# Two graph layers on one core: which pairs' later layers run beside the last sort, and how far ahead their gathered rows are asked for

## The chip, the cores and the metric

One core of a Trainium2 chip runs the whole program. The number that counts is the device time of one execution in microseconds. The engines are named as in the profile: PE is TensorE (matrix products), PEld its weight loads, DVE is VectorE, ACT is ScalarE, POOL is GpSimd and SP is SyncE, which here only issues transfers. A name with a q behind it (SPq, POOLq) is the sequencer of that engine, where DMAs are issued.

## What is computed

Sixteen graphs of 1024 nodes with 64 channels go through two layers. Layer 0 takes the ReLU of a layer norm, drops some edges by a rule on the degree, and takes for every node and channel a weighted sum of three quantiles over the values of its neighbours; a small network with 128 hidden units follows. Layer 1 is three graph convolutions, whose outputs are joined and multiplied once more. Both layers add their result to their input.

```python
def reference(x, adj, nodemask, ...):
    # layer 0
    h = max(layernorm(x), 0)
    nd   = edges of adj left after dropping, with the node itself
    s    = sort(where(nd, h[neighbours], inf))            # per node and channel
    agg  = sum over (tau, w) of w * quantile(s, tau)      # 0.25, 0.5, 0.75
    y    = relu((h + agg) @ W1 + b1) @ W2 + b2
    x    = x + y * mask
    # layer 1
    h  = max(layernorm(x), 0)
    x1 = bn(relu(adj @ (h  @ W1) + b1))
    x2 = bn(relu(adj @ (x1 @ W2) + b2))
    x3 = bn(relu(adj @ (x2 @ W3) + b3))
    x  = x + relu(concat(x1, x2, x3) @ Wl + bl)
```

## The kernel before, in words

The graphs are handled as eight pairs, 0 to 7, two graphs side by side. Three kinds of work follow each other for a pair.

- Preparation: the adjacency is read, edges are dropped, nodes are put in the order of their degree and the places of the nodes in that order are kept in `place`.
- The sort. Nodes in order of degree fall into seven blocks of columns (`BLOCKS`) and a tail. For each block PE gathers the neighbours' values into `g` (line 1018), and DVE runs a network of minima and maxima on it (line 935) and weighs the rows (941, 950). The aggregates are turned by PE (1043), copied by ACT and written to DRAM (`agg_d`), in degree order.
- The later layers, in `later`. `first(p)` is the rest of layer 0. It loads `xt`, `h` and the mask on SP's queue (lines 1240, 1241 and 1249), and gathers the rows of `agg_d` by the indices of `place` with sixteen indirect DMAs of 128 rows on POOL's queue (line 1243). Then DVE adds `agg` and `h` (1142), PE turns the sum (1131) and ACT copies it (1134), two products with ReLU follow for each graph (1151, 1152, 1155, 1156), the mask and the skip connection (1158, 1159), a layer norm (560 to 568, with ACT at 563 and 566), and again a turn into `chan`. `second(p)` is layer 1: it loads the two adjacencies `adjT` (1259), and for each of three convolutions makes the product with the weights (1184), splits it into three bf16 parts (ACT 1185 and 1189, DVE 1188 and 1190), multiplies by the adjacency in two halves of 48 products (1200), and finishes each half on ACT (1204) and DVE (1205). The last product is line 1216, the end is on DVE (1220, 1223), and SP writes the result (1225).

Generators weave these kinds together: `Steps` wraps a generator whose `yield`s are its steps, and `weave(sort, (steps, count, ...))` takes `count` steps spread over the sorting of one block. While the last pair is sorted, `later` is the work that is woven in, with `STEPS` steps for each of the blocks 0 to 7 (the tail is 7; in block 0 the sort of the tails of pairs 4 to 6 comes after). Inside `later`, `second(p)` and `first(p + 1)` take steps in turn, so that the first layer of the next pair lies beside the convolutions of this one. `first` has one step for its loads and four behind them; `second` has eleven. What is left of the eight pairs when the sorting ends is run by `ahead.rest()`, in the same order.

Buffers come from pools. `late` holds one buffer of each tile of the later layers, two of `xt`; `ps_late` holds two of each kind in PSUM. With one `agg`, the gathers of pair p + 1 wait until PE has turned the `agg` of pair p for the second time (1131). A pool that opens over the space of others waits for those that used it.

The build does not keep the order of the source strictly: it lays the instructions of each engine out in a list of its own, moving some ahead of others by its estimate of when they can run. In the trace each engine works through its list from front to back.

Of the kernel before, what the change touches and what calls it, by code (L numbers as in the profile page):

```python
# [10 lines left out]
F32 = mybir.dt.float32  # L11
# [4 lines left out]
U8 = mybir.dt.uint8  # L16
# [3 lines left out]
PSUM = bass.MemoryType.PSUM  # L20
DRAM = bass.MemoryType.DRAM

P = 128
C = 64
# [4 lines left out]
TAUS = ((0.25, 0.25), (0.5, 0.5), (0.75, 0.25))  # L29

SHARES = (10, 9, 17, 24, 20, 13, 0)
STEPS = 7

MAGIC = 8388608.0

# [366 lines left out]
def graph_layers_kernel(ctx: ExitStack, tc: tile.TileContext, ins, out: bass.AP):  # L402
    nc = tc.nc
    x_d, adj_d, mask_d = ins["x"], ins["adj"], ins["nodemask"]
    NB, N, _ = x_d.shape
    NT = N // P
    HALF = 512
    NH = N // HALF
    NP = NB // 2
# [144 lines left out]
    def rows_of(ap):  # L554
        return ap.rearrange("(t p) c -> p t c", p=P)
# [476 lines left out]
    def send(pools, after=None):  # L1032

        for one in waiting:
            store(*one, pools, after)
        waiting.clear()
# [100 lines left out]
    def first_layer(pools, xt, h, agg, mask):  # L1137


        one, ps = pools  # L1140
        X = xt.shape[2]
        nc.vector.tensor_tensor(agg, agg, h, ALU.add)
        oT = channels_first(pools, agg, "chan")
        yield
        for x in range(X):
            rows = slice(x * C, (x + 1) * C)
            hT = one.tile([HID, N], F32, tag="hT", name="hT")
            for hf in range(NH):
                sl = slice(hf * HALF, (hf + 1) * HALF)
                pm = ps.tile([HID, HALF], F32, tag="mm", name="pm1")  # L1150
                nc.tensor.matmul(out=pm, lhsT=w1[rows, :], rhs=oT[rows, sl], start=True, stop=True)
                nc.scalar.activation(hT[:, sl], pm, AF.Relu, bias=b1)
            py = ps.tile([P, NT, C], F32, tag="mm", name="py")
            for t in range(NT):
                nc.tensor.matmul(out=py[:, t, :], lhsT=hT[:, t * P : (t + 1) * P], rhs=w2, start=True, stop=True)
            nc.vector.tensor_tensor(h[:, :, x, :], py, b2[:, None, :].to_broadcast([P, NT, C]), ALU.add)
            yield
        nc.vector.tensor_tensor(h, h, mask[:, :, :, None].to_broadcast([P, NT, X, C]), ALU.mult)
        nc.vector.tensor_tensor(xt, xt, h, ALU.add)
        flat = "p t x c -> p (t x) c"  # L1160
        layernorm_relu(one, agg.rearrange(flat), xt.rearrange(flat), h.rearrange(flat), NT * X)
        yield
        return channels_first(pools, agg, "chan")
# [61 lines left out]
            nc.sync.dma_start(out=rows_of(graphs[x]), in_=res[:, :, x, :])  # L1225
        yield

    def later(pools, done):

        one, ps = pools  # L1230

        def first(p):
            assert p < done.sent
            xt = one.tile([P, NT, 2, C], F32, tag="xt", bufs=2, name="xt")
            h, agg = (one.tile([P, NT, 2, C], F32, tag=k, name=k) for k in ("h", "agg"))
            mk = one.tile([P, NT, 2], U8, tag="mk", name="mk")
            mask = one.tile([P, NT, 2], F32, tag="mask", name="mask")
            for x in range(2):
                b = 2 * p + x
                nc.sync.dma_start(out=xt[:, :, x, :], in_=rows_of(x_d[b]))  # L1240
                nc.sync.dma_start(out=h[:, :, x, :], in_=rows_of(h_d[b][:, :]))
                for t in range(NT):
                    nc.gpsimd.indirect_dma_start(  # L1243
                        out=agg[:, t, x, :],
                        out_offset=None,
                        in_=agg_d[b][:, :],
                        in_offset=bass.IndirectOffsetOnAxis(ap=place[:, b, t : t + 1], axis=0),
                    )
                nc.sync.dma_start(out=mk[:, :, x], in_=mask_d[b])
            yield  # L1250
            nc.vector.tensor_copy(mask, mk)
            cur = yield from first_layer(pools, xt, h, agg, mask)
            return xt, cur

        def second(p, x2, cur):
            adjT = []
            for x in range(2):
                adjT.append(one.tile([P, NT, N], F8, tag=f"adjT{x}", name=f"adjT{x}"))
                nc.sync.dma_start(out=adjT[x], in_=adjT_d[2 * p + x][:, :, :])
            yield  # L1260
            yield from next_layer(pools, [out[2 * p], out[2 * p + 1]], adjT, x2, cur)

        given = yield from first(0)
        for p in range(NP):
            now = Steps(second(p, *given))
            ahead = Steps(first(p + 1)) if p + 1 < NP else None
            while now.step():
                yield
                if ahead is not None and ahead.step():
                    yield  # L1270
            if ahead is not None:
                ahead.rest()
                given = ahead.result
# [146 lines left out]
    with ExitStack() as stack:  # L1420
        keep = stack.enter_context(tc.tile_pool(name="keep", bufs=1))
        pools = (
            stack.enter_context(tc.tile_pool(name="work", bufs=1)),
            stack.enter_context(tc.tile_pool(name="ps", bufs=1, space=PSUM)),
            stack.enter_context(tc.tile_pool(name="rows", bufs=1)),
        )
        last = len(BLOCKS)
        with ExitStack() as inner:
            early = (
                inner.enter_context(tc.tile_pool(name="early", bufs=1)), keep,  # L1430
                inner.enter_context(tc.tile_pool(name="ps_early", bufs=1, space=PSUM)),
            )
            ahead = Steps(prepare(0, early))
            ahead.rest()
            st = ahead.result
            first, *_ = gather_block(st, 0, pools)
            first.rest()
            for p in range(NP - 1):


                def coming(st, p):
                    yield from st.number
                    return (yield from prepare(p + 1, early))

                ahead = Steps(coming(st, p))
                for n in range(last):
                    steps = (ahead, SHARES[n], 0.0, 1.0)
                    if n == 0 and p in TAILS:

                        tails = sort_tails(*TAILS[p], pools)  # L1450
                        next(tails)
                        weave(sort_block(st, n, pools), steps)
                        weave(tails, gather_block(st, n + 1, pools))
                    elif n == last - 1:
                        ahead.rest()
                        to_come = ahead.result
                        weave(sort_block(st, n, pools), gather_block(to_come, 0, pools))
                    elif n == last - 2:
                        weave(
                            sort_block(st, n, pools), gather_block(st, n + 1, pools),  # L1460
                            gather_block(st, last, pools, (early[0], "a", 2)), steps,
                        )
                    else:
                        weave(sort_block(st, n, pools), gather_block(st, n + 1, pools), steps)
                st = to_come
            for _ in st.number:
                pass


        with ExitStack() as inner:  # L1470
            one = inner.enter_context(tc.tile_pool(name="late", bufs=1))
            late = (one, inner.enter_context(tc.tile_pool(name="ps_late", bufs=2, space=PSUM)))
            done = Pair()
            done.sent = TAILS[NP - 1][0]
            ahead = Steps(later(late, done))
            for n in range(last + 1):
                steps = (ahead, STEPS, 0.0, 1.0)
                if n == 0:
                    tails = sort_tails(*TAILS[NP - 1], pools)
                    next(tails)  # L1480
                    weave(sort_block(st, n, pools), steps)
                    weave(tails, gather_block(st, n + 1, pools))
                    continue
                if n < last:
                    weave(sort_block(st, n, pools), gather_block(st, n + 1, pools), steps)
                else:
                    weave(sort_block(st, n, pools), steps)
                done.sent = NP - 1
            send(pools)
            done.sent = NP  # L1490
            ahead.rest()


    with ExitStack() as stack:
# [43 lines left out]
```

## Time and profile before

| what | us |
|---|---|
| three runs: median (lowest, highest) | 3160.63 (3157.54, 3173.24) |
| the profiled execution: its own time | 3163.56 |
| its span | 3161.8 |
| preparation and sorts of pairs 0 to 6, up to the sort of the last pair | 0 to about 2340 |
| last sort, with the later layers beside it | about 2340 to 2832.2 |
| later layers alone | 2832.2 to 3161.8 |

Results of pairs 0 to 7 are issued to DRAM at 2623.7, 2736.2, 2823.0, 2900.0, 2972.7, 3048.1, 3108.8 and 3155.0 us. So three pairs are finished beside the sort; the fourth is in its first convolution when the sort ends and the fifth in its first layer.

The times of the trace are microseconds from the start of the span; a line of the timeline gives start, duration, engine, line of the code, operation, names, how many, and in brackets the idle time of the engine ahead of it with the work that ended it. A line of the waits says which engine at which line waited for which, the total, how often, and the longest.

### The profile page before, as it was taken

The page shows a single profiled execution, that of the slowest core. Times are in us where ns is not written, and L with a number is a line of the kernel's source. Part 1 is how long each engine was busy: PE and PEld are TensorE (multiplying, and loading weights), DVE is VectorE, ACT ScalarE, POOL GpSimd, SP SyncE. Part 2 cuts the span into 40 slices and gives each one's busy share as a digit, 9 for nine tenths or more (in the row PEclk, how much of TensorE's full clock was granted, in tenths as well). Part 3 has the DMA queues.
Part 4 walks back from the last instruction along what each step waited for, and adds up shares of the span by engine and source line. Part 5 has one row for each costly group of instructions (what it writes and reads, how often), then busy time and mean ns, then how long its engine had stood idle before and what let it go on. Part 6 is the DMA issues. An engine that isn't in the chain of part 4 may idle for free.

```text
span 3161.8 us, 67201 instructions
## 1 busy us (share of the span) xinstructions
PE 2599.2 (82%) x27849; PEld 1697.4 (54%) x27849; DVE 2559.8 (81%) x5895; ACT 1696.2 (54%) x3292; POOL 619.5 (20%) x545
## 2 busy tenths in 40 slices
PE   2678978898888889885798889888986688977778
PEld 1445655565556556653565566456643456644445
DVE  4149889998999799989998999899976979963332
ACT  4764666567557755774367557745853223332221
POOL 5110161022102200330022103300422530311110
PEclk9779999999899999997899999999987799988989
DMA  4131022111211212122111211211113011122211
GB/s 138 46 104 60 3 67 70 56 55 52 66 57 54 64 56 68 46 72 47 42 64 51 66 56 57 67 56 63 48 36 75 9 41 26 49 55 54 54 54 42
DMA packets 221082, 177.45 MB, mean 56 GB/s; under 512 B 189024, under 2 KB 189152, under 8 KB 216672
## 3 DMA queue, kind: packets, MB, share of 16 engines
q1 hardware_dynamic: 141824, 125.88, 13.1%
q0 software_dynamic: 17408, 37.81, 3.9%
q10 hardware_dynamic: 61536, 9.39, 1.7%
q8 instruction: 219, 3.59, 0.5%
q14 instruction: 95, 0.78, 0.1%
HBM read 124.44 MB, written 48.55 MB: 55 GB/s over the span
## 4 chain that ended last, share of the span: by engine, by line
DVE 40%; PE 29%; ACT 12%; DMA 8%; issue 6%; another core or an unknown queue 2%; POOL 2%; ACTq 1%; DVEq 0%; POOLq 0%; SPq 0%
PE pg L1018 11%; DVE t L935 10%; DVE s L987 9%; DVE g L935 8%; PE pg L1200 5%; ACT junk L770 3%; DMA a<-in_adj 3%; DMA lp<-live_d 3%; DVE junk_v L673 2%; PE pr L845 2%; DVE g_tails L935 1%; DVE t_tails L935 1%; PE keys L763 1%; PE pf L1216 1%
## 5 line engine op out<-in xcount | busy, mean ns | idle before, releaser
L1018 PE MATMUL pg<-s,hp 128*64 128x400 bf16 (+11 forms) x16848 | 1366.5, 313 | 172.3 <-DVE s L987 138.1
L1018 PEld LDWEIGHTS <-hp 128*64 128x64 bf16 x16848 | 894.5, 112 | 553.9 <-issue 109.6
L987 DVE TENSOR_SCALAR s<-r 128x3200 bf16<-128x3200 bf16 (+25 forms) x1312 | 623.6, 521 | 103.6 <-PE pg L1018 74.9
L778 POOL DMA_INDIRECT live_d<-edge,place x128 | 261.1, 2040 | 1354.3 <-DVE place L773 1149.9
L1023 ACT COPY g<-pg 128x400 f32<-128x400 f32 (+10 forms) x384 | 169.0, 443 | 399.4 <-PE pg L1018 363.1
L935 DVE TENSOR_TENSOR t<-g 128x600 f32<-128x600 f32 (+9 forms) x524 | 315.5, 626 | 34.0 <-ACT g L1023 33.2
L1200 PE MATMUL pg<-adjT,xw 128*64 128x512 fp8e4 x2304 | 284.5, 398 | 52.8 <-ACT xw L1185 25.7
L935 DVE TENSOR_TENSOR g<-t 128x96 f32<-128x96 f32 (+16 forms) x555 | 283.2, 537 | 1.2
L1243 POOL DMA_INDIRECT agg<-agg_d,place x128 | 171.2, 1338 | 495.2 <-PE pt L1131 258.2
L671 ACT ACTIVATE edge<-a 128x1024 fp8e4<-128x1024 f32 x128 | 135.1, 1058 | 214.4 <-DMA a<-in_adj 213.9
L1200 PEld LDWEIGHTS <-xw 128*64 128x64 bf16 x2304 | 140.1, 114 | 182.4 <-issue 42.0
L868 ACT ACTIVATE coef<-z,bias 128x200 f32<-128x200 bf16 (+6 forms) x480 | 173.9, 405 | 102.3 <-DVE agg L950 66.0
L935 DVE TENSOR_TENSOR t<-t 128x192 f32<-128x192 f32 (+20 forms) x447 | 207.8, 475 | 0.2
L871 ACT ACTIVATE coef<-coef,wcol 128x200 f32<-128x200 f32 (+7 forms) x512 | 189.6, 403 | 9.3 <-issue 7.1
L673 DVE SCALAR_TENSOR_TENSOR junk_v<-a 128x1024 fp8e4<-128x1024 f32 x128 | 155.4, 1214 | 24.4 <-DMA a<-in_adj 24.4
L845 PE MATMUL pr<-liveT,upto 128*128 128x512 fp8e4 (+2 forms) x384 | 127.4, 350 | 53.1 <-ACT r L851 46.9
L770 ACT ACTIVATE junk<-keys,minus 128x1024 fp8e4<-128x1024 f32 x128 | 144.3, 1128 | 38.1 <-PE keys L763 34.3
L851 ACT CAST r<-pr 128x592 bf16<-128x592 f32 (+1 forms) x256 | 142.5, 585 | 41.1 <-PE pr L847 32.1
L794 POOL DMA_DIRECT2D lp<-live_d x128 | 89.4, 699 | 376.9 <-PE pt L809 319.3
L812 ACT ACTIVATE liveT<-pt 128x1024 fp8e4<-128x1024 f32 x128 | 130.3, 1034 | 50.5 <-PE pt L809 47.1
L752 ACT ACTIVATE edge<-q,bias 128x1024 fp8e4<-128x1024 f32 x128 | 141.8, 1108 | 22.6 <-PE q L747 22.6
L725 ACT ACTIVATE stays<-cs,back 128x1024 f16<-128x1024 f32 x128 | 136.7, 1111 | 31.1 <-PE cs L721 15.9
(182 smaller groups left out, 3879.4 us busy)
## 6 DMA issues: line engine op xcount, KB each, us to landing
a<-in_adj SPq DMA_DIRECT2D x128, 512.0 KB
adjT_d<-edgeT SPq DMA_DIRECT2D x16, 1024.0 KB
lp<-live_d POOLq DMA_DIRECT2D x128, 128.0 KB
adjT<-adjT_d SPq DMA_DIRECT2D x16, 1024.0 KB
room<-in_x SPq DMA_DIRECT2D x16, 256.0 KB
h_d<-room SPq DMA_DIRECT2D x16, 256.0 KB
h_again<-h_d SPq DMA_DIRECT2D x16, 256.0 KB
xt<-in_x SPq DMA_DIRECT2D x16, 256.0 KB
```

The costliest lines, as they stand in the source:

```text
L673: nc.vector.scalar_tensor_tensor(junk, a, 1.0, a, ALU.is_equal, ALU.not_equal, accum_out=odd[:, b, t : t + 1], saturate=False)
L770: nc.scalar.activation(junk, keys, AF.Sign, bias=minus[:, t : t + 1], accum_out=above[:, t : t + 1], saturate=False)
L778: sent = nc.gpsimd.indirect_dma_start(out=live_d[b][:, :], out_offset=bass.IndirectOffsetOnAxis(ap=place[:, b, t : t + 1], axis=0), in_=ed ...
L845: nc.tensor.matmul(out=pr[:, o], lhsT=upto, rhs=liveT[:, u, sl], start=True, stop=(u == 0))
L868: nc.scalar.activation(coef[:, i, :], z[:, at], AF.Abs, bias=bias(rank - (slots + 1) // 2 + tau), scale=sign)
L871: nc.scalar.activation(coef[:, i, :], coef[:, i, :], AF.Relu, bias=wcol[:, q : q + 1], scale=-w)
L935: nc.vector.tensor_tensor(view(bufs, o, n1, n2), view(bufs, a, n1, n2), view(bufs, b, n1, n2), ALU.max if op else ALU.min)
L987: nc.vector.tensor_scalar(s[:, k, :, us, w0:], r[:, :, us, at + w0 : at + W], float(LIVE + 1 + k0 + k), None, ALU.is_equal)
L1018: summed = nc.tensor.matmul(out=pg[x * C : (x + 1) * C, ks, w0:], lhsT=st.hp[:, part, x, u, :], rhs=s[:, ks, x, u, w0:], start=(whole and ...
L1023: nc.scalar.copy(g[:, k0 : k0 + n, :], pg)
L1200: nc.tensor.matmul(out=pg[cs, :], lhsT=part[:, u, cs], rhs=adjT[x][:, u, sl], start=(u == 0 and k == 0), stop=(u == NT - 1 and k == len(xw ...
L1243: nc.gpsimd.indirect_dma_start(out=agg[:, t, x, :], out_offset=None, in_=agg_d[b][:, :], in_offset=bass.IndirectOffsetOnAxis(ap=place[:, b ...
```

## The change

Four things change. `STEPS` goes from 7 to 11, but in block 0 of the last sort only one step is taken. `first` puts `LEAD` = 4 empty steps between its loads with the gathers and the first use of them. Only pairs 0 to 3 (`BESIDE`) are given to the `later` beside the sort, and `ahead.rest()` ends them there. Pairs 4 to 7 get a `later` of their own, after the pools of the sort are closed: new pools (`last` with two buffers of each tile and four of `xt`, `h`, `agg` and the mask's bytes, `ps_last` with four PSUM buffers of each kind), in which two series, pairs 4 and 6 and pairs 5 and 7, take steps in turn. In a series (`in_turn`) the loads of the next pair are issued before the layers of this one, and `first` and `second` of one pair follow each other.

```diff
-STEPS = 7
+STEPS = 11
+BESIDE = 4
+LEAD = 4
@@ later
-    def later(pools, done):
+    def later(pools, done, pairs, apart=False):
         one, ps = pools
-        def first(p):
+        deep = dict(bufs=4) if apart else {}
+        def load(p):
             assert p < done.sent
-            xt = one.tile([P, NT, 2, C], F32, tag="xt", bufs=2, name="xt")
-            h, agg = (one.tile([P, NT, 2, C], F32, tag=k, name=k) for k in ("h", "agg"))
+            xt = one.tile([P, NT, 2, C], F32, tag="xt", bufs=4 if apart else 2, name="xt")
+            h, agg = (one.tile([P, NT, 2, C], F32, tag=k, name=k, **deep) for k in ("h", "agg"))
...
-            yield
+            return xt, h, agg, mk
+
+        def first(p, loaded=None):
+            if loaded is None:
+                loaded = load(p)
+                for _ in range(LEAD):
+                    yield
+            xt, h, agg, mk = loaded
+            mask = one.tile([P, NT, 2], F32, tag="mask", name="mask")
             nc.vector.tensor_copy(mask, mk)
             cur = yield from first_layer(pools, xt, h, agg, mask)
             return xt, cur
...
-        given = yield from first(0)
-        for p in range(NP):
+        def in_turn(pairs):
+            ahead = load(pairs[0])
+            yield
+            for i, p in enumerate(pairs):
+                loaded, ahead = ahead, load(pairs[i + 1]) if i + 1 < len(pairs) else None
+                yield from second(p, *(yield from first(p, loaded)))
+
+        if apart:
+            both = [Steps(in_turn(pairs[k::2])) for k in range(2)]
+            while any([one.step() for one in both]):
+                yield
+            return
+        given = yield from first(pairs[0])
+        for p in pairs:
             now = Steps(second(p, *given))
-            ahead = Steps(first(p + 1)) if p + 1 < NP else None
+            ahead = Steps(first(p + 1)) if p + 1 in pairs else None
@@ the last sort
-            ahead = Steps(later(late, done))
+            ahead = Steps(later(late, done, range(BESIDE)))
             for n in range(last + 1):
-                steps = (ahead, STEPS, 0.0, 1.0)
+                steps = (ahead, STEPS if n else 1, 0.0, 1.0)
...
             send(pools)
-            done.sent = NP
             ahead.rest()
+    with ExitStack() as stack:
+        done.sent = NP
+        late = (
+            stack.enter_context(tc.tile_pool(name="last", bufs=2)),
+            stack.enter_context(tc.tile_pool(name="ps_last", bufs=4, space=PSUM)),
+        )
+        Steps(later(late, done, range(BESIDE, NP), True)).rest()
```

More of the change, by code (lines that the diff above doesn't have):

```diff
@@ L1226, in next_layer @@
         yield
-    def later(pools, done):
+    def later(pools, done, pairs, apart=False):
         one, ps = pools
-        def first(p):
+        deep = dict(bufs=4) if apart else {}
+        def load(p):
             assert p < done.sent
-            xt = one.tile([P, NT, 2, C], F32, tag="xt", bufs=2, name="xt")
-            h, agg = (one.tile([P, NT, 2, C], F32, tag=k, name=k) for k in ("h", "agg"))
-            mk = one.tile([P, NT, 2], U8, tag="mk", name="mk")
-            mask = one.tile([P, NT, 2], F32, tag="mask", name="mask")
+            xt = one.tile([P, NT, 2, C], F32, tag="xt", bufs=4 if apart else 2, name="xt")
+            h, agg = (one.tile([P, NT, 2, C], F32, tag=k, name=k, **deep) for k in ("h", "agg"))
+            mk = one.tile([P, NT, 2], U8, tag="mk", name="mk", **deep)
             for x in range(2):
```

## The prediction

> **What bounds the kernel now.** I read the page's totals first, then the waits in two stretches, then the timelines of PE and POOL. The totals name no single bound, since stages differ:
>
> ```profile
> PE 2599.2 (82%) x27849; PEld 1697.4 (54%) x27849; DVE 2559.8 (81%) x5895; ACT 1696.2 (54%) x3292; POOL 619.5 (20%) x545
> ```
>
> The change touches only what follows 2340 us, so I split there. Beside the last sort (2350 to 2834) DVE's own waits are:
>
> ```profile
> DVE agg L1142 <- DMA agg<-agg_d,place: 22.6, 2, 12.6
> DVE xT L1205 <- ACT xT L1204: 18.1, 5, 6.0
> DVE h L1156 <- PE py L1155: 14.1, 6, 5.7
> ```
>
> DVE is the bound there: from 2340 to 2834 all its waits together are 85 us, and the sort's instructions fill the rest. After the sort (2834 to 3162) PE is the bound, with gaps. The windows (columns: PE, PEld, DVE, ACT, POOL busy, then clock and DMA) show a pair with gathers beside it, and one without:
>
> ```profile
> 3006.00:3029.00 23.00, 11.99 (x72) 6.22 (x71) 1.93 (x3) 2.63 (x5) 15.12 (x16) 0.65 0.10 24
> 3080.00:3103.00 23.00, 22.50 (x184) 16.17 (x184) 4.65 (x8) 5.54 (x9) 0.00 (x0) 0.93 0.04 9
> ```
>
> PE halves its work while POOL gathers. The last product of each pair gives the pace:
>
> ```profile
> 2892.40 5.62 PE L1216 MATMUL pf<-wlast,xT 128*128 128x128 f32 x48
> 2965.09 5.62 PE L1216 MATMUL pf<-wlast,xT 128*128 128x128 f32 x48
> 3040.47 5.62 PE L1216 MATMUL pf<-wlast,xT 128*128 128x128 f32 x48
> 3101.16 5.62 PE L1216 MATMUL pf<-wlast,xT 128*128 128x128 f32 x48
> 3147.31 5.62 PE L1216 MATMUL pf<-wlast,xT 128*128 128x128 f32 x48
> ```
>
> The steps are 72.7, 75.4, 60.7 and 46.2 us: with gathers beside, twice; with a first layer but no gathers; alone. So gathers cost about 13 us a pair here and a hidden first layer 14.5. Last, POOL's gathers: the first one of pair 2, beside the sort, and the ends of a set there and of one after the sort.
>
> ```profile
> 2568.96 8.27 POOL L1243 DMA_INDIRECT agg<-agg_d,place  x1 [74.07 <-DVE s L987]
> 2599.25 0.94 POOL L1243 DMA_INDIRECT agg<-agg_d,place  x1 [0.30 <-DMA agg<-agg_d,place]
> 2856.72 0.94 POOL L1243 DMA_INDIRECT agg<-agg_d,place  x1 [57.91 <-PE pt L1131]
> 2875.44 0.95 POOL L1243 DMA_INDIRECT agg<-agg_d,place  x1 [0.30 <-issue]
> ```
>
> Sixteen take 31 us beside the sort (47 for pair 1, 2449.7 to 2497) and 20 after it, 0.94 with 0.30 between.
>
> [...] 1.57 us a gather beside the sort, 0.94 when DVE idles. [...] Here the last gather of pair 0 starts at 2412.47 and DVE goes on at 2415.12, 2.65 us later. [...] four products take 3.71 us at 2418 after a pause, 1.98 at 2916.
>
> **The change part by part.** For the changed kernel I have the lists in which its instructions stand on each engine, and what each waits for, but no times; lines are those of before. Up to the end of the last sort DVE's list holds the same work in both (117 instructions of the later layers before, 116 now: pairs 0 to 2, pair 3 up to its first convolution).
>
> 1. *End of the sort*, 2832.2 before. (a) Pair 0's first layer moves behind the tails' sort: its two waits at line 1156, 3.61 and 5.74 us, go: -9.4. (b) Pair 4's gathers leave this stretch; in 2778 to 2800 DVE was busy 9.8 of 22 us: -12.2. (c) The gathers' waits. The four empty steps don't lengthen the way from release to use: a pair's 19 steps now fill under two blocks, and the release (line 568, then PE's turn 1131) comes late in the pair. Summing DVE's list between line 568 of one pair and line 1142 of the next, at the trace's durations for each shape (0.25 us at 96 columns, 0.98 at 800, linear between), gives 21.7, 18.1 and 23.3 us for pairs 1, 2 and 3; before it was 50.1, 34.5 and 42.6. Against 30 to 47 us of gathers that leaves 5 to 19 us (PE is loaded there and covers part), 15 and 8; pair 0 keeps about 10, since its sum stands right behind its gathers as before. About 45 in place of 22.6: +22. Net 0, with ±20: -46 if every gather wait goes (a, b and all of 22.6), +20 if none of (b) is found.
>
> 2. *Pair 3 alone.* Before, pair 4's first layer lay beside it. Now nothing does: the first loads of the new pools wait for PE's last product of pair 3 and for the landing of its two result stores. From the second convolution on, pair 7 before took 34 us (3121.45 to 3154.95), and stores land about 4.5 us after issue (DMA engines are busy until some 3159.4). 38.7 in all.
>
> 3. *Gathers of pairs 4 to 7.* All 64 stand back to back on POOL, none issued before step 2 ends. 64 x 1.25 = 80, and 2.4 to land. Beside them SP brings 16 loads of 256 KB and four adjacencies of 1 MB; with such loads pair 0's sixteen took 23 us instead of 20, so up to 10 more. I take 86 (82 to 92). What waits: DVE's list has the sum (line 1142) of pair 6 ahead of the second output half of pair 4's first layer, and the sum of pair 7 ahead of pair 4's and 5's variance (565) and normalising (568). DVE can't pass it, so PE gets no convolution until pair 7's rows have landed, although only pairs 4 and 5 need theirs (at 20 and 40 us). The first layers of 4 and 5, some 20 us of PE, are hidden in these 86.
>
> 4. *Chain behind it*: DVE 1.22 + 1.21 + 1.22 + 0.25 + 1.22, PE's turns 1.0, ACT 0.6 twice, the same for pair 5 interleaved, products 1184 and ACT 1185: 11.
>
> 5. *Convolutions of 4 and 5 together.* Twelve halves at 5.4 (the x48 groups of line 1200 at full clock) are 64.8; two later rounds of line 1184, 4.6 each, 9.2; line 1216 twice, 11.3; 2 for a cold start: 87. Handoffs of one pair lie under the other's products; alone a pair would take 46.2.
>
> 6. *First layers of 6 and 7.* They follow line 1216 in PE's list with nothing beside. PE: turns 2.1, then 8 us a pair, 19 with ACT; then DVE's 0.69, eight of 1.2 and small ones, 13, turn and products 3: 35.
>
> 7. *Convolutions of 6 and 7*: 87. *End*: 9.5 (8.9 from line 1216 before).
>
> Sum behind the sort: 38.7 + 86 + 11 + 87 + 35 + 87 + 9.5 = 354. Before: 3161.8 - 2832.2 = 329.6. With step 1 at 0 that is +24.6 on the span. The profiled execution took 3163.56, of which 1.8 lie outside the span, and the median of the three runs is 2.9 below it; I add the difference to the median: 3160.6 + 24.6, about 3185.
>
> **Rivals.** *R1, the gathers' waits lengthen the sort.* For: the short distances of 1c. Against: PE's load may cover them. +20 more: 3205. *R2, the hold at pair 7's rows costs little.* Pair 5 lands at 42 us, its own chain takes 35, so convolutions could not start before 79 in place of 97: -18, 3167, no difference that can be told. For it: DMA could run quicker than I take; against: the list. *R3, faster: rows asked for ahead leave the last sort.* One mechanism, DVE's idle time from 2390 to 2800: if the waits at 1142 (22.6), 1156 (9.4) and in pair 4's window (12.2) all go, the sort ends 44 us sooner: 3141. It decides once it removes more than 40 us (24.6 + 15.8). For: (a) and (b) are sure to move; against: 1c.
>
> **How the numbers follow.** Under 0.5%, 15.8 us, a change in this kernel can't be told from none. Forecast 0.49 (3172 to 3200), R1 0.25, R2 0.18, R3 0.08. Slower: 0.86 of the forecast (0.42), all of R1, a tenth of R2: 0.69. Same: the rest of the forecast and of R2: 0.07 + 0.16 = 0.23. Faster: 0.08. The range takes in R2, R1 with its waits somewhat longer than 20 us, and part of the way to R3: 3154 to 3216.
>
> **What would show it.** After pair 3's result a stretch of some 85 us with PE mostly idle, POOL issuing 64 gathers in a row, and DVE waiting at line 1142 for `agg_d` rows of pairs 6 and 7; then two dense stretches of PE of about 85 us with 35 between them; gathers' waits on DVE beside the sort above 22.6. I am wrong if PE's convolutions start within 60 us of pair 3's store, if the sort ends before 2800, or if POOL's gathers after it take well off 1.25 us.

## The result, and the profile after

The changed kernel is slower. Its median over four runs is 3211.41 us (3205.90 to 3222.38), against 3161.79 (3157.54 to 3173.24) for the kernel before beside it: a ratio of 1.0146, with a 95% interval of 1.0123 to 1.0168. The forecast of 3185 lay 26 us below, and the range (3154 to 3216) holds the result near its upper end.

In the profiled execution (span 3207.2 us, 45.4 more than before) the last sort ends 7.0 us sooner (2825.9 against 2832.8, by the end of PE's last `pt_agg`), and what follows takes 381.3 us instead of 329.0. In code, lines of the later layers now stand four below the old ones, those of the loads six.

Beside the sort, the view of the waits (2340 to 2826; total, times, longest) shows DVE waiting longer for gathered rows:

```profile
DVE agg L1146 <- DMA agg<-agg_d,place: 37.9, 4, 11.5
DVE h L1160 <- PE py L1159: 16.8, 5, 6.9
```

These are the 22.6 and 14.1 of before. Behind the sort the windows show four stretches of the tail (columns as in the prediction):

```profile
2863.00:2898.90 35.90, 9.53 (x28) 6.29 (x28) 1.63 (x3) 2.54 (x4) 26.95 (x28) 0.50 0.81 141
2898.90:2940.30 41.40, 0.00 (x0) 0.00 (x0) 0.03 (x1) 0.00 (x0) 30.56 (x34) 0.50 0.37 128
2940.30:2996.00 55.70, 33.09 (x116) 22.49 (x116) 22.31 (x28) 12.10 (x20) 4.20 (x4) 0.53 0.01 3
2996.00:3066.00 70.00, 70.00 (x641) 39.68 (x640) 20.20 (x33) 18.85 (x32) 0.00 (x0) 1.00 0.06 22
```

For 41.4 us POOL is the only engine that works, issuing gathers. The timeline of that place names the two ends of the hole, and the sums of pairs 6 and 7 after it:

```profile
2863.72 0.94 POOL L1249 DMA_INDIRECT agg<-agg_d,place  x1 [120.99 <-DMA out<-res]
...
2896.91 1.97 PE L1159 MATMUL py<-w_L_gnn_W,hT 128*128 128x64 f32 x8 [0.75 <-issue]
...
2940.28 0.69 DVE L1160 TENSOR_TENSOR h<-py,r_L_gnn_b 128x512 f32<-128x512 f32 x1 [51.90 <-remote]
...
2942.15 1.97 PE L1135 MATMUL pt<-ident,agg 128*128 128x128 f32 x8 [43.27 <-DVE agg L1146]
2943.22 0.94 POOL L1249 DMA_INDIRECT agg<-agg_d,place  x1 [0.30 <-issue]
2944.47 0.94 POOL L1249 DMA_INDIRECT agg<-agg_d,place  x1 [0.30 <-issue]
2950.78 0.58 ACT L1138 COPY chan<-pt 128x512 f32<-128x512 f32 x1 [53.91 <-remote]
...
2962.76 1.21 DVE L1146 TENSOR_TENSOR agg<-agg,h 128x1024 f32<-128x1024 f32 x1
...
2983.26 1.22 DVE L1146 TENSOR_TENSOR agg<-agg,h 128x1024 f32<-128x1024 f32 x1
```

PE's products `py` of pair 4 should end at 2898.88 by the record, whose ends are modelled. DVE's addition, which waits in the program for these products and for nothing later, starts at 2940.28; "remote" means that no event in the profile explains the moment. The raw record of PE's semaphore agrees with DVE: the update stands at 2940.25. ACT's copy of the next turn is late in the same way, 8.6 us behind the turn's start. The sums of pairs 6 and 7, for whose rows the prediction had DVE waiting, run without any idle time ahead of them.

| stretch (us) | predicted | profiled |
|---|---|---|
| sort's end to the first gather | 38.7 | 37.8 |
| first gather to the first convolution | 86 + 11 = 97 | 132.3 |
| convolutions of 4 and 5 | 87 | 81.0 |
| first layers of 6 and 7 | 35 | 37.5 |
| convolutions of 6 and 7 | 87 | 81.0 |
| end | 9.5 | 11.6 |

One term is wrong by much. The experiments ask why.

### The profile page after: what moved, and what is told of

The parts are those of the page before. It is cut to its first block, busy times and chain, and to the rows that moved or that the text cites. A ratio compares the mean times of both kernels' runs of the same rounds, so it can differ in the third digit from the quotient of the medians.

```text
span 3207.2 us, 67200 instructions
## 1 busy us (share of the span) xinstructions
PE 2601.9 (81%) x27826; PEld 1710.8 (53%) x27849; DVE 2561.1 (80%) x5895; ACT 1693.9 (53%) x3292; POOL 578.3 (18%) x545
## 4 chain that ended last, share of the span: by engine, by line
DVE 43%; PE 26%; ACT 11%; DMA 7%; issue 6%; POOL 3%; another core or an unknown queue 2%; SPq 1%; ACTq 1%; DVEq 0%; POOLq 0%
DVE t L939 11%; DVE s L991 10%; DVE g L939 9%; PE pg L1022 8%; PE pg L1204 5%; ACT junk L774 3%; DMA lp<-live_d 3%; DVE junk_v L677 3%; POOL agg L1249 2%; DMA a<-in_adj 2%; DVE g_tails L939 1%; DVE t_tails L939 1%; PE pr L849 1%; DVE coef L945 1%
## 5 line engine op out<-in xcount | busy, mean ns | idle before, releaser
L782 POOL DMA_INDIRECT live_d<-edge,place x128 | 243.8, 1905 | 1349.7 <-DVE place L777 1145.3
L1204 PE MATMUL pg<-adjT,xw 128*64 128x512 fp8e4 x2304 | 261.4, 381 | 6.8 <-issue 3.0
L1249 POOL DMA_INDIRECT agg<-agg_d,place x128 | 149.1, 1165 | 439.1 <-PE pt L1135 248.7
L774 ACT ACTIVATE junk<-keys,minus 128x1024 fp8e4<-128x1024 f32 x128 | 144.3, 1128 | 37.7 <-PE keys L767 34.6
```

What stands on the lines that cost most here:

```text
L774: nc.scalar.activation(junk, keys, AF.Sign, bias=minus[:, t : t + 1], accum_out=above[:, t : t + 1], saturate=False)
L782: sent = nc.gpsimd.indirect_dma_start(out=live_d[b][:, :], out_offset=bass.IndirectOffsetOnAxis(ap=place[:, b, t : t + 1], axis=0), in_=ed ...
L1204: nc.tensor.matmul(out=pg[cs, :], lhsT=part[:, u, cs], rhs=adjT[x][:, u, sl], start=(u == 0 and k == 0), stop=(u == NT - 1 and k == len(xw ...
L1249: nc.gpsimd.indirect_dma_start(out=agg[:, t, x, :], out_offset=None, in_=agg_d[b][:, :], in_offset=bass.IndirectOffsetOnAxis(ap=place[:, b ...
```

## The experiments

They ran on three chips, here A, B and C; which chip the first comparison used isn't known. Each ratio is to the kernel before on the same chip.

| run | chip | median, us | kernel before | ratio (95%) |
|---|---|---|---|---|
| tail_direct | A | 3115.92 | 3129.15 | 0.9970 (0.9952 to 0.9989) |
| tail_unused | A | 3123.16 | 3129.15 | 0.9982 (0.9966 to 0.9998) |
| tail_load_behind | A | 3145.39 | 3129.15 | 1.0055 (1.0040 to 1.0069) |
| one_series | A | 3134.38 | 3129.15 | 1.0007 (0.9991 to 1.0023) |
| after_again | B | 3219.14 | 3175.76 | 1.0124 (1.0095 to 1.0154) |
| before_again | B | 3175.20 | 3175.76 | 0.9995 (0.9979 to 1.0010) |
| apart_only | B | 3212.31 | 3175.76 | 1.0111 (1.0064 to 1.0159) |
| early_rows | B | 3131.33 | 3175.76 | 0.9877 (0.9847 to 0.9907) |
| after_third | C | 3210.34 | 3165.43 | 1.0166 (1.0127 to 1.0206) |
| tail_unused_2 | C | 3210.45 | 3165.43 | 1.0141 (1.0098 to 1.0185) |
| tail_direct_2 | A | 3115.55 | 3129.03 | 0.9954 (0.9935 to 0.9974) |
| early_rows7 | A | 3062.68 | 3129.03 | 0.9778 (0.9751 to 0.9805) |

**No gathers in the tail.** In `load`, pairs 4 to 7 read their aggregates directly:

```diff
+                if apart:
+                    nc.sync.dma_start(out=agg[:, :, x, :], in_=rows_of(agg_d[b][:, :]))
+                else:
                     for t in range(NT):
                         nc.gpsimd.indirect_dma_start(
...
```

> The changed kernel, but pairs 4 to 7 read their aggregates as they lie in DRAM, with direct loads on SP's queue, instead of 64 indirect gathers on POOL's (this leaves out putting their rows back into the order of the nodes; all other work is kept). The changed kernel spends 132 us from its first gather to the first convolution of pairs 4 and 5. Theory 1 (hand-overs from PE to DVE and ACT are held up while POOL issues indirect DMAs) and theory 2 (the predicted hold: the sums of pairs 6 and 7 stand in DVE's list, and their rows are late) both expect that stretch to fall to about 45 us (the loads, and 37.6 us for two first layers as measured for pairs 6 and 7), so some 85 us less: about 3125 us. Theory 3 (the first layers of 4 and 5 are slow for a reason of their own, such as the new pools or a slow PE after the idle time) expects over 90 us there and 3170 us or more.

The stretch from the first load to the first convolution took 69.2 us, not 45: two first layers at half clock with loads ahead of them are dearer than I took (PE is busy for 42.7 us of it at a granted clock of 0.52; the first layers of 6 and 7 in the changed kernel took 26.8 us of PE at 0.82). That is 64 us less than the 133.0 of the changed kernel, also counted from the first load, as theories 1 and 2 want, though on another chip.

**64 gathers that nobody reads.** The direct loads stay, and the gathers fill a spare tile:

```diff
+                if apart:
+                    nc.sync.dma_start(out=agg[:, :, x, :], in_=rows_of(agg_d[b][:, :]))
+                    if x == 0:
+                        spare = one.tile([P, NT, 2, C], F32, tag="spare", name="spare", **deep)
                 for t in range(NT):
-                        out=agg[:, t, x, :],
+                        out=(spare if apart else agg)[:, t, x, :],
```

> As the run before it (pairs 4 to 7 read their aggregates directly, rows not put in order), but the 64 gathers are issued all the same at the same place, into tiles that nothing reads. Nothing waits for their data. Theory 1 (gathers in flight hold up PE's hand-overs) expects the first convolution of pairs 4 and 5 some 100 to 130 us behind the first gather, with DVE or ACT starting 5 to 40 us after the PE work that they wait for: 3180 to 3211 us. Theory 2 (waiting for rows in DVE's list) expects the same time as with direct loads alone, about 3125 us, within 10 us.

On chip A the stretch was 68.8 us and the ratio 0.998: theory 2's numbers. Theory 1 seemed dead. The timeline of this run on A shows DVE starting 0.04 us behind PE's modelled end of 2866.48, gathers on both sides:

```profile
2862.81 3.67 PE L1159 MATMUL py<-w_L_gnn_W,hT 128*128 128x64 f32 x16
...
2865.63 0.94 POOL L1253 DMA_INDIRECT spare<-agg_d,place  x1 [0.30 <-issue]
2866.52 0.69 DVE L1160 TENSOR_TENSOR h<-py,r_L_gnn_b 128x512 f32<-128x512 f32 x1 [8.70 <-PE py L1159]
2866.87 0.94 POOL L1253 DMA_INDIRECT spare<-agg_d,place  x1 [0.30 <-issue]
...
2868.40 1.97 PE L1135 MATMUL pt<-ident,agg 128*128 128x128 f32 x8 [1.92 <-DVE agg L1146]
...
2869.55 0.59 ACT L1138 COPY chan<-pt 128x512 f32<-128x512 f32 x1 [5.95 <-PE pt L1135]
```

**Loads of 6 and 7 behind the first layers of 4 and 5.**

```diff
-                loaded, ahead = ahead, load(pairs[i + 1]) if i + 1 < len(pairs) else None
-                yield from second(p, *(yield from first(p, loaded)))
+                given = yield from first(p, ahead)
+                ahead = load(pairs[i + 1]) if i + 1 < len(pairs) else None
+                yield from second(p, *given)
```

> The changed kernel, but in each series of the tail the next pair's loads and gathers are issued behind the first layer of this pair, not ahead of it. All work is kept. 32 gathers (32 x 1.25 = 40 us) then stand ahead of the first layers of 4 and 5. Theory 1 expects the convolutions of 4 and 5 to start about 40 + 45 = 85 us behind the first gather instead of 132 (47 us less), but the other 32 gathers then run beside the start of those convolutions and hold up their hand-overs, which gives back 10 to 40 us: 3165 to 3205 us. Theory 2 expects the 47 us and nothing given back, as the sums of 6 and 7 come late in DVE's list: about 3165 us. If the two first layers are slow by themselves (theory 3), 3200 us or more.

The first convolution came 97.1 us behind the first load, and no start was late by "remote". On this chip, waiting for the rows of 4 and 5 thus costs 28 us over direct loads (97.1 - 69.2); the changed kernel, on another chip, needed 36 more than that. The 3145 us lie below every time expected: those were set from the 3211 of the first comparison, and the kernel before takes 3129 here. The edit also does less than its text says. `agg` has four buffers, so nothing on POOL's queue waits, and all 64 gathers run in a row (2833.7 to 2916.8), not in two lots; only the order of SP's loads and, a little, DVE's list changed. So this is nearly the changed kernel on chip A, with 64 gathers beside the first layers, and PE's work is handed over in time.

**Only the part beside the sort.** `BESIDE` goes from 4 to all eight pairs and the block with the pools of its own is taken out:

```diff
-            ahead = Steps(later(late, done, range(BESIDE)))
+            ahead = Steps(later(late, done, range(NP)))
...
-    with ExitStack() as stack:
-        done.sent = NP
...
-        Steps(later(late, done, range(BESIDE, NP), True)).rest()
```

> Only the part of the change that lies beside the last sort: 11 steps a block, one in block 0, four empty steps behind the loads; the tail is left as in the kernel before, one series of all eight pairs with the pools beside the sort, no pools of its own. All work is kept. If that part is good by itself, the sort ends near 2825 us as in the changed kernel, pair 3 is stored near 2865 instead of 2900, and pairs 4 to 7 follow as before in 262 us: about 3130 us, faster than both. If the steps beside the sort only move waits (rival), the sort ends later than 2832 or pair 4 loses what pair 3 won: 3155 to 3170 us.

1.0007: the rival's side (the 3134 us look like the gain that was expected, but the kernel before takes 3129 on this chip). Pair 3 is stored at 2876.3, and the next two pairs still take 72 us each, since DVE waits for rows of the next pair (shown below).

**The changed kernel and the kernel before, unaltered.** The runs so far left it open whether the late starts belong to the order of work or to the chip.

> The changed kernel itself, unaltered, on the chip of the four runs before. There, no start of DVE or ACT behind PE came late, neither with 64 gathers whose rows nobody reads (0.998 of the kernel before) nor with gathers in two lots (1.006), so theory 1, that gathers in flight hold up the hand-overs by themselves, has lost its ground. Theory 4 (the late hand-overs belong to the chip or the execution of the first comparison, in which the kernel before shows them too): DVE's first addition of py starts within 1 us of PE's products; pair 5's rows (32 gathers, 40 us and about 3 to land) still hold up its first layer, so the first convolution starts about 95 us behind the first gather (the 69 us of the run with direct loads, and some 30 for rows that come late): ratio 1.003 to 1.008. Theory 5 (the waits for rows in this very order bring the late hand-overs about): again about 132 us and a ratio of 1.014 to 1.018.

> The kernel before, unaltered, for its profile on this chip. Ratio 1.000 within 0.002. Theory 4 expects none of the late starts of ACT behind PE (4 to 12 us each, some 12 to 15 us for a pair) that its first profile shows at pairs 4, 5 and 6 after the sort, and so about 35 us less after the sort than the 329.6 us of the first profile. Theory 5 expects them again, at the same places.

Chip B has the late starts: 1.0124 for the changed kernel, again 133.0 us from first load to first convolution, with DVE's addition 40.7 us late. The kernel before has the late starts too; the waits behind its sort (2849 to 3178) say

```profile
ACT xT L1204 <- remote: 30.7, 3, 11.7
ACT xw L1185 <- remote: 21.6, 5, 6.4
...
DVE agg L1142 <- DMA agg<-agg_d,place: 0.8, 1, 0.8
```

and each of them lies inside a set of gathers or within 4 us of its last one. Theory 4's time for the kernel before (35 us less behind the sort) was a miss: 329.1 us against 329.0. Theory 5 came nearest here; the ratio lies just below its 1.014.

**Only the tail part of the change.**

```diff
-STEPS = 11
-LEAD = 4
+STEPS = 7
+LEAD = 1
-                steps = (ahead, STEPS if n else 1, 0.0, 1.0)
+                steps = (ahead, STEPS, 0.0, 1.0)
```

> Only the part of the change that lies behind the sort: pairs 4 to 7 in two series with pools of their own, loads one pair ahead; beside the sort the 7 steps a block of the kernel before and no empty steps. All work is kept. As 7 steps bring pair 3 only to its first convolution by the sort's end, pair 3 runs alone for about 65 us instead of 38.4 before the tail's first load: the ratio is 0.008 to 0.010 above that of the changed kernel. If the steps beside the sort matter little, as the run with one series (1.001) says of them, the same as the changed kernel within 0.003.

1.0111 beside 1.0124 of the whole change on the same chip, the same within their intervals: the loss sits in the tail. My price for the missing steps was a miss: the sort ended at 2819.4 and the first gather started at 2862.7, 43 us on its own, not 65. DVE's addition is 41 us late again, and the stretch takes 133.2 us.

**The decisive pair.** The changed kernel and the unused gathers, side by side on chip C:

> The changed kernel, unaltered, once more, beside the run that follows. On the second chip it was 1.012 of the kernel before, again with DVE's addition of py some 42 us late behind PE; on the first chip of the experiments no kernel had such late starts, and the kernel before took 3129 us there instead of 3161 to 3176. If this chip is of the kind of the second (the kernel before near 3165 or above): 1.010 to 1.017, with the late start again. If it is of the kind of the first (near 3130): theory 4 expects no late start and 1.003 to 1.008; theory 5 the late start all the same and 1.012 or more.

> The run with 64 gathers whose rows nobody reads and direct loads for pairs 4 to 7 (their rows are not put in order), once more, beside the changed kernel on the same chip. If the kernel before is near 3165 us or above here, this decides theory 1 for such a chip: with gathers in flight that hold up PE's hand-overs by themselves, some of DVE's or ACT's starts come 4 us and more behind PE's work and the ratio to the kernel before is 1.005 or more; if it is the wait for rows that matters, none does and the ratio is 0.985 to 0.998. If the kernel before is near 3130 us: 0.998 again.

The same program that ran at 0.998 on A runs at 1.0141 on C, level with the changed kernel (3210.45 and 3210.34 us). Its timeline on C:

```profile
2902.82 3.84 PE L1159 MATMUL py<-w_L_gnn_W,hT 128*128 128x64 f32 x16
...
2944.66 0.69 DVE L1160 TENSOR_TENSOR h<-py,r_L_gnn_b 128x512 f32<-128x512 f32 x1 [47.12 <-remote]
...
2946.54 1.97 PE L1135 MATMUL pt<-ident,agg 128*128 128x128 f32 x8 [39.88 <-DVE agg L1146]
...
2955.86 0.59 ACT L1138 COPY chan<-pt 128x512 f32<-128x512 f32 x1 [51.22 <-remote]
...
2965.11 0.95 POOL L1253 DMA_INDIRECT spare<-agg_d,place  x1 [0.30 <-issue]
2967.06 0.59 ACT L1138 COPY chan<-pt 128x512 f32<-128x512 f32 x1 [10.61 <-remote]
2967.70 2.07 PE L1155 MATMUL pm<-chan,w_L_gnn_W 64*128 64x512 f32 x2 [9.13 <-issue]
2971.97 0.69 ACT L1156 ACTIVATE hT<-pm,c_L_gnn_b 128x512 f32<-128x512 f32 x1 [4.33 <-remote]
2972.71 1.97 PE L1159 MATMUL py<-w_L_gnn_W,hT 128*128 128x64 f32 x8 [2.94 <-ACT hT L1156]
```

DVE starts 38.0 us behind PE's modelled end where on A it was 0.04, though nothing here waits for a gather. Lateness lasts until some 7 us after the last gather's start, and then PE and ACT follow each other as on A. So waiting for rows is not needed for it, against theory 5: the late start (38.0 us on C, 0.04 on A) comes with gathers that nobody reads too, on one chip and not on the other. The changed kernel beside it on C has the late start as well; its first convolution comes 132.5 us behind the first load.

> The run with direct loads for pairs 4 to 7 and no gathers behind the sort (their rows are not put in order), once more. On the third chip the 64 unused gathers alone brought the late hand-overs back (1.014 there, 0.998 on the first chip). If this chip is of that kind (the kernel before near 3165 us or above): should gathers be the cause, there is no late start here, the first convolution of pairs 4 and 5 starts about 70 us behind the first load and the ratio is 0.980 to 0.988; should any DMA traffic of that stretch (8 MB of loads stay) do it, DVE's addition of py is late by 10 us or more and the ratio is 1.00 or more. If the kernel before is near 3130 us here, 0.997 again, which tells nothing new.

This run fell on A again and told nothing new. Whether direct loads alone are free of late starts on B or C, that is, whether the gathers or all the traffic of the stretch cause them, wasn't measured by a run. The traces on record speak for the gathers. In the kernel before on B all late starts lie at gathers. And in the changed kernel's first profile the last packet of SP's loads ends at 2914.1; from there to 2946.6 only packets of gathers move, and yet the turn of pair 5, which starts at 2942.15, is handed over late. The same holds on B (loads end at 2932.5, the turn starts at 2959.17) and for the unused gathers on C (2942.7 and 2946.54).

**Rows a pair ahead.** If gathers must not stand just ahead of what needs them, they can be issued a pair sooner, with a second `agg` (the gathers of pair 0 get a step of their own):

```diff
-        res = one.tile([P, NT, X, C], F32, tag="res", name="res")
+        res = one.tile([P, NT, X, C], F32, tag="hT", name="res")
...
+        def rows(p):
+            agg = one.tile([P, NT, 2, C], F32, tag="agg", bufs=2, name="agg")
...
         def first(p):
+            if p + 1 in pairs:
+                gathered.append(rows(p + 1))
+            agg = gathered.pop(0)
```

> A version to beat both: one series of eight pairs, 11 steps a block, but two buffers of agg, and the gathers of pair p + 1 issued when the first layer of pair p begins, not when its own does; the result tile takes the place of hT to make room. All work is kept. In the run with one series DVE waits 12.7, 13.5 and 11.5 us for the rows of pairs 5, 6 and 7 after the sort. If these waits were on the path, as theory 2 and the predicted hold in DVE's list have it, 30 to 40 us less: ratio 0.987 to 0.991. If PE has other work behind them (rival), 0.997 to 1.000.

> The version to beat both, but with the 7 steps a block of the kernel before beside the sort: the kernel before with two buffers of agg and the gathers issued one pair ahead, and nothing else (the result tile takes the place of hT). All work is kept. With 11 steps it was 0.988 on the second chip. If the 11 steps are worth nothing by themselves, as the run with one series (1.001) says, 0.985 to 0.991; if they carry the gain, 0.996 to 1.000.

0.9877 on B and, with 7 steps, 0.9778 on A: faster than the kernel before on both chips, and on B than the changed kernel (1.0124). On A it is more than the 0.985 to 0.991 that was expected. As the two ran on different chips, they don't say what 11 steps cost against 7. The waits show where it comes from on A, first `one_series`, then `early_rows7`; beside the sort (2340 to 2860):

```profile
DVE agg L1146 <- DMA agg<-agg_d,place: 47.0, 5, 11.6
```

```profile
DVE agg L1146 <- DMA agg<-agg_d,place: 10.8, 2, 10.6
```

and behind it:

```profile
DVE agg L1146 <- DMA agg<-agg_d,place: 37.7, 3, 13.5
```

```profile
DVE agg L1146 <- DMA h<-h_d: 4.4, 3, 1.6
```

and SP's result stores from pair 3 on, again `one_series` first (the second column is the time over all issues of the line; the last line holds pairs 6 and 7):

```profile
2876.34 1.01 SPq L1229 DMA_DIRECT2D out<-res  x2
2948.84 1.01 SPq L1229 DMA_DIRECT2D out<-res  x2
3020.65 1.01 SPq L1229 DMA_DIRECT2D out<-res  x2
```

```profile
2831.56 1.02 SPq L1229 DMA_DIRECT2D out<-res  x2
2892.25 1.01 SPq L1229 DMA_DIRECT2D out<-res  x2
2951.39 1.02 SPq L1229 DMA_DIRECT2D out<-res  x2
3012.08 47.27 SPq L1229 DMA_DIRECT2D out<-res  x4
```

Pairs 4 and 5 take 60 us each instead of 72: the wait for rows, 12.6 us in the mean, is gone. That is the smaller part. Of the 70.9 us between the two spans 45 lie ahead of pair 3's store, where DVE waits 36 us less for rows beside the sort, and 26 behind it. All waits for rows went from 84.7 to 10.8 us, with 4.4 for `h` in addition, which comes near the whole; but the two runs differ in their steps as well, so this is a balance and not a proof.

On B the late starts are not gone. At the last two sets of gathers in `early_rows` ACT starts by "remote" four times, behind idle times of 11.1, 9.5, 5.0 and 5.0 us. Pair 4 takes 77 us and pair 5 takes 59; most of the gain, 49 us in the profiles, lies ahead of pair 3's store (2866.9 against 2916.2 in the kernel before on B). Up to the sort's end DVE's waits for rows fell only from 22.7 to 11.4 us there, which doesn't account for it; what does stays open.

## Why the prediction was right, and where not

The sign and the place were right, and the range held the result, in part by luck: its upper end was made for longer waits beside the sort, which ended sooner instead. As foretold came two dense stretches of convolutions with the first layers of 6 and 7 bare between them, pair 3 alone for 38 us, and all 64 gathers behind one another at 1.25 us. DVE's wait at the sums of pairs 6 and 7, which the prediction named as a sign, did not come. `apart_only` shows that the loss lies in that tail.

*Step 1, the sort's end.* Predicted 0, within 20; it came 7.0 us sooner. The gathers' waits beside the sort rose to 37.9, near the 45 expected, and `one_series` (1.0007) shows that the part beside the sort is worth nothing by itself.

*Steps 3 and 4 are what failed.* The term is "the first layers of 4 and 5, some 20 us of PE, are hidden in these 86", with DVE held by the sums of pairs 6 and 7: 97 us predicted, 132.3 measured. The hold at those sums never decided: the first layers of 4 and 5 weren't done when the last rows landed. Their 20 us of PE were too few by half, 42.6 us busy at a granted clock of 0.51. And the products `py` of pair 4 were handed over 41.4 us late on the first chip, 40.7 on B, a cost that the prediction put at nothing. Measured from the first load, 133.0 us splits so against the 68.8 of the unused gathers on A: 12.9 later start of `py`, since pair 4's rows come by 16 gathers (31.2 us against 18.3); 1.0 in `py` itself; 41.4 until DVE's addition; 9.0 more from pair 5's turn to the first convolution (53.9 against 44.9). Pair 5's rows landed inside the 41.4. `tail_unused_2` shows on C that late hand-overs alone bring the loss (126.9 us with no row waited for), and `tail_load_behind` on A that without them the rows of 4 and 5 bring 97.1: my 97, by luck, with the wrong reason behind it.

*Steps 5 and 7* were 6 us too long each. In the trace a half takes 5.2 us, not 5.4, and the round's products 3.8, not 4.6; the 2 us for a cold start, my estimate, did not show: the clock of this stretch (2996 to 3077) is 1.00. In the kernel before, four products of line 1151 took 3.71 us at a clock of 0.50 (at 2418) and 1.98 at 1.00 (at 2916). Step 6 and the end were 2 us short each, step 2 was 0.9 too long. Together these give 8 us back of the 35 lost in steps 3 and 4.

The rivals: R2 needed convolutions some 79 us behind the first gather, and no run that gathers its rows had them before 96; R3 needed the sort's waits to go, and they grew; with a second `agg`, in `early_rows7`, they went (47.0 to 10.8). R1's number came nearest to the result, but not by its mechanism, as the sort ended sooner. Some of the prediction's small sums don't come out of their own terms: the two ends of step 1 give -44 and +13, not -46 and +20, step 2 gives 38.0, and R2's 42 and 35 give 77. None of this changes the forecast by more than 1 us.

The warning stood on the page: before, "PE halves its work while POOL gathers". I took it for a price of 13 us a pair, and then let PE work beside 64 gathers at no price. The waits of the kernel before behind its sort (2834 to 3162) named it too:

```profile
ACT xT L1204 <- remote: 29.3, 3, 11.7
```

On A that price is DVE's wait for rows (37.7 us for three pairs); on B it is PE's late hand-overs (ACT idles 52.3 us ahead of them in the kernel before, PE's usual time included, and DVE 0.8 for rows).

## What to carry to other kernels

Gathered rows belong a whole unit of work ahead of their use, behind a second buffer: here that took 0.9778 of the time before on A and 0.9877 on B. A burst of gathers right ahead of the work that opens a stage can hold this work beyond its own end: in the first profile 82 us of gathers stood ahead of convolutions that began 132 us behind the first of them, and products beside them were handed over 41.4 us late. Two series that start together bare their first layers together: what one series hides is then on the path (37.5 us for pairs 6 and 7). And a cause that falls in an experiment on one chip may stand on another (the unused gathers: 0.9982 on A, 1.0141 on C): compare the changed kernel itself on the same chip before dropping a theory.

## What the runs showed of the hardware

The program with unused gathers had spans of 3124.2 us on A and 3222.5 on C. Of the 98 us, 40.3 had gathered by the sort's end (2807.3 and 2847.6), 58.1 lie between the first load and the first convolution, and what follows takes 210.9 and 210.8. Behind the gathers the two chips run alike; why they differ by 40 us up to the sort's end is not shown.

Whether PE's work is late or only its signal, the record of PE's semaphore tells in part. The turn of pair 5 is eight products, each of which raises it by one. On A, in `tail_load_behind`, the updates stand 0.21 us apart (2885.08 to 2886.57), with gathers under way. In the changed kernel's first profile they stand at 2943.75, 2946.55, 2949.35, 2950.75, 2952.15, 2952.85, 2953.55 and 2953.59: 2.80 us apart, then 1.40, then 0.70, while the last gather starts at 2944.47. ACT's two copies start at 2950.78 and 2953.61, right behind the fourth and the eighth. B has the same spacings (2960.76, 2963.57, 2966.36, 2967.76, 2969.17, 2969.86), and ACT's first copy starts there at 2967.79, behind the fourth. So no single signal is lost: products are handed over one by one, at first at a thirteenth of A's pace (2.80 us against 0.21), and in this profile the pace doubles in steps within some 9 us of the last gather's start. An estimate from this: sixteen products `py` at 2.80 us would take 44.8, and from their first start to the update it was 46.1 in the first profile and 41.8 on C. What sets the slow pace off stays open. The first turn of pair 4 in the first profile (2888.6) was handed over in time, though gathers had then run for 25 us.

Where `py` of pair 4 stands, the windows give a granted clock of 0.50 on A (`tail_unused`, 2844.5 to 2866.5), on C (`tail_unused_2`, 2884.8 to 2906.7) and in the first profile (2863 to 2898.9), so the recorded clock doesn't tell the chips apart: by the record `py` takes 3.67 us on A and 3.84 on C, and DVE follows 0.04 and 38.0 us behind it. No run shows what holds PE's products back on B and C. The ends of matmuls in the trace are modelled and show nothing of it.

Left open: what differs between the chips, and the changed kernel on A, which was not run there. My estimate for it is about the 1.0055 of `tail_load_behind`, where the same gathers run in the same row.
